# Layer 1 of a conv-attention hybrid: token sums of chunks added during the attention units, and work moved between the two linear parts

## The chip, the cores and the metric

The kernel runs on one core of one Trainium2 chip. The metric is the device time in microseconds of one execution, and the number compared is the median of several runs.

## What is computed

The input is eight images of 384 channels and 32 x 32 positions, that is 1024 tokens of 384 numbers per image. Layer 0 normalises groups of channels and adds an attention of 8 heads with a relative bias. Layer 1, which the change touches, works on the tokens of layer 0's output:

```python
t = t + attn(_ln_t(t))        # 6 heads of 64; q and k normalised per head and token
t = t + ffn(_ln_t(t))         # 384 -> 1536 -> 384, gelu between, both linear parts quantised

def _ln_t(v, eps=1e-5):
    m = jnp.mean(v, axis=-1, keepdims=True)
    s = jnp.var(v, axis=-1, keepdims=True)
    return (v - m) / jnp.sqrt(s + eps)
...
for g in range(NUM_GROUPS):   # 5 groups over 8 images: one image each, the last three give zero
    gamma = jnp.max(jnp.abs(ag))
    xq = xq.at[...].set(jnp.clip(ag * QB / (gamma + EPS), -QB + EPS, QB - EPS))
```

So only images 0 to 4 have a feed-forward part; for images 5 to 7 it adds nothing, and the kernel leaves it out. The normalisation of tokens (`_ln_t`) needs, for each token, the sum over 384 channels of the values and of their squares. The quantisation of the first linear part needs the largest absolute value of the whole image before gelu can start.

## The kernel before

An image lies in SBUF channel by channel: three chunks of 128 channels on the partitions, 1024 tokens along each row. A sum over channels is therefore a sum over partitions and chunks, and the kernel makes it on TensorE, with a matrix of ones as the weights (`token_sums`, L1112 to L1130). For each of the three chunks it multiplies x and the square of x, each in two halves of 512 tokens. The four results use 32 columns of the array each. All three chunks accumulate in one PSUM tile. In f32 every such product shows as two matmul records. ScalarE makes the squares (`square`, L1107). The sums go through DRAM into a layout with tokens on the partitions (two DMAs on SyncE's queue, SP), and GpSimd makes mean and scale from them (`token_stats`, L1133).

There are two such sums per image: the a-sum ("tsa") on the image that comes next, for its attention, where only the scale is needed, and it is applied to v late; and the f-sum ("tsf") on the image after its attention, for the feed-forward part.

The attention of an image runs in 24 units (3 pairs of heads x 2 halves of the queries x 4 groups of keys, L1611). In each unit TensorE makes scores (`scores`, L1286), ScalarE takes exp of them, and VectorE adds up the exps for the softmax's divisor. Two units later (`LAG`) TensorE multiplies them with v (`weigh`, L1331). When a pair of heads is done, `divide` (L1359) sums over keys, inverts, spreads the result by DMA ("rb") and multiplies the output oT by it.

Between the units of two images lies a seam. After images 5 and 6 the seam holds only the next image's projections (`attention_inputs`, L1583): the a-sum, q and k of three pairs, the last units' products, and four quarters of v, which VectorE scales with the a-sum's result as it takes them from PSUM (L1240). The output projection of the old image follows behind unit 3 of the next.

After images 0 to 4 the seam holds much more, written out by hand in the main loop from L1671 on. In TensorE's order: the four quarters of v for the next image (`project_v`, L1225) with the last products between them; the output projection (`project_out`, L1395), whose last pair needs rb; q of pair 0 (`project(0, 0)`); the f-sum, the a-sum; k of pair 0, q of pair 1, sums of q and k over each head (`head_sums`, L1173), k of pair 1; the first linear part ("y1p", L1481), 12 row blocks of 12 matmuls; q and k of pair 2; the second linear part ("y2p", L1538), 12 steps k of 12 matmuls. Both linear parts work on two float32r parts of each value, a high and a low one. For the first, `layer_norm` (L1421) makes them on VectorE and ScalarE after the f-sum has gone through DRAM and GpSimd. For the second, `Supply.gelu` and `Supply.split` (L1522 to L1533) make them on ScalarE and VectorE, chunk by chunk, once `quant_scale` has the largest value.

`normalise_qk` (L1186) turns head sums into scales: SP loads them, GpSimd takes a power, SP stores them and loads the k scales; after `steps[0]` more steps SP spreads the q scales ("rq"), and `steps[1]` steps later VectorE multiplies q by them.

Three things set the order. Each engine runs its instructions in the order in which the program issues them. `_Later` (L64) keeps work that is due after so many calls of `step()`; a call comes after each unit, each projection, each row block and each step k, and what is due is issued there. And buffers are few: PSUM has four tiles of 128 x 1024 for everything (`mm2`, L111), and the f32 work tiles of that size (`wtile`) are 16.

Of the kernel before, what the change touches and what calls it, by code (L numbers as in the profile page):

```python
# [27 lines left out]
P = 128  # L28
# [3 lines left out]
KC = C // P  # L32
# [998 lines left out]
def _layer1(tc, ins, x1, out, shared, start, before=None, check=None):  # L1031
# [4 lines left out]
    with ExitStack() as ctx:  # L1036
# [75 lines left out]
        def token_sums(name, xt, sqs):  # L1112

            pst = mm2("ts" + name)
            for k in range(KC):
                for i, s in enumerate((xt[:, k], sqs[k])):
                    for h in range(NH):
                        nc.tensor.matmul(
                            pst[ts(2 * i + h, 32), 0], ones[:, 0:32], s[:, ts(h, HALF)],
                            start=(k == 0), stop=(k == KC - 1),  # L1120
                        )
# [21 lines left out]
        def project_qk(b, pair, s, xt, dst, sq, step=True):  # L1143
# [3 lines left out]
            for k in range(KC):  # L1147
                for h in range(NH):
                    nc.tensor.matmul(  # L1149
                        pq[:, h], wqkv[:, k, s * C + pair * P : s * C + (pair + 1) * P],  # L1150
                        xt[:, k, ts(h, HALF)], start=(k == 0), stop=(k == KC - 1),
                    )
# [72 lines left out]
        def project_v(b, xt, m2, c=None):  # L1225
# [9 lines left out]
            if c is None:  # L1235
                nc.vector.tensor_copy(v[:, 2 * m2 : 2 * m2 + 2], pv[:, :, 0:C])
# [158 lines left out]
        def project_out(b, oT, xt, then):  # L1395

            pps = []
            for pairs in (range(NP1 - 1), range(NP1 - 1, NP1)):
                for m in range(KC):
# [81 lines left out]
        def feed_forward_1(b, un, between):  # L1481
# [17 lines left out]
            for m in range(FC):  # L1499
# [7 lines left out]
                if m == 4:  # L1507
                    between()
            top = largest(f"1_{b}", parts)
            quant_scale(top)  # L1510
            return y1, top
# [26 lines left out]
        def feed_forward_2(b, supply, between, xt):  # L1538
# [10 lines left out]
            for k in range(FC):  # L1549
                supply.split(k + 1)  # L1550
                supply.gelu(k + 2)
# [3 lines left out]
                between(k)  # L1555
                later.step()
# [26 lines left out]
        def attention_inputs(b, xt, rest=()):  # L1583
# [3 lines left out]
            tk = token_sums(f"a{b}", xt, [square(f"a{b}", xt, k) for k in range(KC)])  # L1587
# [40 lines left out]
        for b in range(B):  # L1628
# [9 lines left out]
            for i, u in enumerate(units):  # L1638
# [7 lines left out]
                if i == 3:  # L1646
# [4 lines left out]
                    ahead = load(b + 1) if more else None  # L1651
            if not more:
# [6 lines left out]
            if not ffn:  # L1659

                def last(i, b=b, oT=oT, held=held):
                    weigh_last(b, oT, held[i])
                    if i == 1:
                        divide(b, oT, NP1 - 1)

                nqk, nkc = attention_inputs(b + 1, ahead, [lambda: last(0), lambda: last(1)])
# [3 lines left out]
            else:  # L1670
                nqk, sq, d, nkc = {}, {}, head_rows(b + 1), kc_tile(b + 1)  # L1671
                sqs = [square(f"a{b + 1}", ahead, k) for k in range(KC)]

                def project(pair, s, step=True):
# [122 lines left out]
```

## Time and profile before

| what | us |
|---|---|
| median of 3 runs (lowest 3085.49, highest 3087.35) | 3085.55 |
| the profiled execution | 3085.19 |
| its span, from first to last instruction | 3083.4 |
| TensorE busy with matmuls | 3039.7 |
| VectorE, ScalarE, GpSimd busy | 1736.9, 1400.0, 472.1 |
| layer 1's first matmul of a token sum starts at | 1434.1 |

A line of the profile's timeline gives the start in us, the us that the entry spans, the engine (PE is TensorE, DVE VectorE, ACT ScalarE, POOL GpSimd, SP SyncE), the source line, the operation, the tiles written and read, their shapes and the number of instructions. A bracket at its end gives the time that the engine stood idle before it and who ended that. A matmul's record is longer than the pace of the matmuls, since the next one starts before its end: 128 x 512 f32 records have a mean of 596 ns and start 0.43 us apart. So a busy TensorE can still hold small losses, and they are read from the starts.

TensorE's longest waits for a named releaser in layer 1, over the whole span (us, times, longest):

```
PE y2p L1544 <- DVE ly L1533: 5.3, 9, 0.7
PE hs L1178 <- ACT qsq L1165: 3.3, 5, 0.7
PE y2p L1544 <- ACT qsq L1165: 3.0, 5, 0.6
PE pp L1404 <- DVE oT L1390: 2.4, 1, 2.4
PE s L1293 <- DVE v L1240: 2.2, 2, 1.2
PE y1p L1490 <- ACT qsq L1165: 2.2, 5, 0.4
PE y1p L1490 <- DVE lun L1444: 2.1, 5, 0.4
PE tsa L1118 <- ACT tsqa L1109: 1.5, 2, 0.8
```

### The profile page before, as it was taken

The numbers are of one execution on the slowest core, as the hardware profiler recorded it, in microseconds if no ns is written. First come the engines' busy times: TensorE is split into PE (matmuls) and PEld (weight loads), VectorE is DVE, ScalarE is ACT, GpSimd is POOL, SyncE is SP. The second block draws the span as 40 slices with busy tenths as digits, with TensorE's granted clock in tenths as the row PEclk, the third lists the DMA queues.
The fourth block names the chain that finished last, engine by engine and source line by source line (L and its number), as shares of the span: only waits on it lengthen the run. The fifth ranks groups of instructions, "written<-read, shape, count | busy, mean of one in ns | idle before, by whom it ended". The sixth has DMA issues, their size and how long they took to land.

```text
span 3083.4 us, 45983 instructions
## 1 busy us (share of the span) xinstructions
PE 3039.7 (99%) x19066; PEld 1582.6 (51%) x19066; DVE 1736.9 (56%) x1735; ACT 1400.0 (45%) x1763; POOL 472.1 (15%) x315
## 2 busy tenths in 40 slices
PE   8999999999999999999999999999999999999998
PEld 3455546454555546444545555645645645634343
DVE  3846547273646547263645845745745745745545
ACT  2634426162434526153644643543643544544534
POOL 0111102011111102032201301201201201211110
PEclk9999999999999999999999999999999999999999
DMA  7402020202112020213301101101101101102011
GB/s 185 115 19 82 20 80 23 82 18 50 51 25 82 19 81 23 57 66 95 81 15 30 56 15 30 57 15 30 57 15 30 57 15 30 57 9 73 14 51 44
DMA packets 102771, 150.51 MB, mean 49 GB/s; under 512 B 62260, under 2 KB 65828, under 8 KB 101784
## 3 DMA queue, kind: packets, MB, share of 16 engines
q1 hardware_dynamic: 99688, 147.41, 16.8%
q8 instruction: 153, 2.51, 0.3%
q14 instruction: 66, 0.54, 0.1%
q10 hardware_dynamic: 2864, 0.05, 0.1%
HBM read 111.05 MB, written 27.32 MB: 45 GB/s over the span
## 4 chain that ended last, share of the span: by engine, by line
PE 87%; DVE 4%; DMA 3%; ACT 2%; issue 1%; SPq 1%; POOL 1%; DVEq 0%; ACTq 0%; POOLq 0%
PE s L521 14%; PE o L552 14%; PE s L1293 11%; PE o L1342 10%; PE pq L467 8%; PE y2p L1544 5%; PE pp L616 4%; PE y1p L1490 4%; PE pp L1404 4%; PE pv L495 4%; PE pq L1149 4%; PE pv L1230 3%; SPq L391 1%; PE sum L1365 1%; POOL hc L1199 1%
## 5 line engine op out<-in xcount | busy, mean ns | idle before, releaser
L536 ACT ACTIVATE e<-e 128x1024 f32<-128x1024 f32 x512 | 535.0, 1057 | 442.7 <-DVE e L532 422.1
L532 DVE TENSOR_TENSOR e<-s,grow 128x1024 f32<-128x1024 f32 x512 | 601.4, 1218 | 190.4 <-PE s L521 189.8
L521 PE MATMUL s<-qk 48*64 48x512 f32 x4096 | 612.4, 592 | 2.7 <-DVE e L532 2.6
L552 PE MATMUL o<-e,v 64*64 64x512 f32 x4096 | 608.3, 590 | 0.0
L1304 ACT ACTIVATE e<-s,kc 128x512 f32<-128x512 f32 x768 | 463.4, 691 | 200.1 <-PE s L1293 183.9
L1293 PE MATMUL s<-qk,qk 64*64 64x512 f32 x3072 | 393.1, 592 | 2.4 <-DVE v L1240 2.2
L1342 PE MATMUL o<-e,v 64*64 64x512 f32 x3072 | 390.8, 591 | 0.0
L521 PEld LDWEIGHTS s<-qk 48*64 48x64 f32 x4096 | 237.0, 132 | 228.5 <-issue 76.3
L552 PEld LDWEIGHTS o<-e,v 64*64 64x64 f32 x4096 | 259.6, 133 | 178.4 <-issue 71.1
L1319 DVE TENSOR_TENSOR t<-t,e 128x1024 f32<-128x1024 f32 x192 | 231.1, 1222 | 75.3 <-ACT e L1304 75.2
L1149 PE MATMUL pq<-bx,wqkv 128*128 128x512 f32 x576 | 254.1, 596 | 0.7 <-ACT tra L1123 0.7
L467 PE MATMUL pq<-xn,w 128*128 128x512 f32 x576 | 250.7, 596 | 0.0
L581 POOL TENSOR_TENSOR inv<-sums,over 128x16 f32<-128x16 f32 x32 | 92.7, 2898 | 1008.7 <-DMA sums<-sd 850.1
L1293 PEld LDWEIGHTS s<-qk,qk 64*64 64x64 f32 x3072 | 142.8, 132 | 200.2 <-issue 124.3
L1342 PEld LDWEIGHTS o<-e,v 64*64 64x64 f32 x3072 | 137.4, 133 | 192.7 <-issue 165.8
L467 PEld LDWEIGHTS pq<-xn,w 128*128 128x128 f32 x576 | 109.2, 191 | 142.3 <-issue 139.5
L1149 PEld LDWEIGHTS pq<-bx,wqkv 128*128 128x128 f32 x576 | 107.8, 190 | 143.5 <-issue 141.4
L1316 DVE TENSOR_TENSOR t<-e,e 128x1024 f32<-128x1024 f32 x96 | 114.1, 1224 | 71.4 <-ACT e L1304 71.2
L1477 DVE TENSOR_REDUCE parts<-y 128x1 f32<-128x1024 f32 x75 | 90.1, 1218 | 99.1 <-ACT y L1474 98.6
L1165 ACT ACTIVATE qsq<-pq 128x1024 f32<-128x1024 f32 x48 | 49.1, 1024 | 195.5 <-DVE qk L1159 97.3
L1199 POOL TENSOR_TENSOR hc<-hc,rsqrt 128x32 f32<-128x32 f32 x24 | 135.4, 5642 | 2.0
L1230 PE MATMUL pv<-wqkv,bx 128*128 128x384 f32 x384 | 131.0, 497 | 0.0
(151 smaller groups left out, 2936.6 us busy)
## 6 DMA issues: line engine op xcount, KB each, us to landing
rb<-rd SPq DMA_DIRECT2D x112, 256.0 KB
xn<-in_x_dram SPq DMA_DIRECT2D x24, 512.0 KB
res<-in_x_dram SPq DMA_DIRECT2D x24, 512.0 KB
x<-res SPq DMA_DIRECT2D x24, 512.0 KB
bx<-x SPq DMA_DIRECT2D x8, 1536.0 KB
rq<-hi SPq DMA_DIRECT2D x48, 256.0 KB
out_dram<-bx SPq DMA_DIRECT2D x24, 512.0 KB
wide<-table SPq DMA_DIRECT2D x80, 114.2 KB
```

The source lines that it names most:

```text
L467: nc.tensor.matmul(pq[:, h], wqk[:, k, s, 2 * pair : 2 * pair + 2, :].rearrange("p h d -> p (h d)"), xn[:, k, ts(h, HALF)], start=(k == 0) ...
L521: nc.tensor.matmul(s[j][ts(c, QP), i], qk[pair][rows, 1, ts(4 * m2 + 2 * i + c, QP)], qk[pair][rows, 0, ts(h, HALF)], start=True, stop=True,)
L532: nc.vector.tensor_add(e.rearrange("p (i q) -> p i q", i=2), s[j], bass.AP(near.tensor, near.offset, [near.ap[0], [-QROWS * IW, 2], [1, HA ...
L536: nc.scalar.activation(e, e, AF.Exp)
L552: nc.tensor.matmul(po[ts(j, S0), r], v[keys, 2 * m2 + i, 2 * pair + j, :], es[j][keys, ts(i, HALF)], start=(m2 == 0 and i == 0), stop=(m2 ...
L1149: nc.tensor.matmul(pq[:, h], wqkv[:, k, s * C + pair * P : s * C + (pair + 1) * P], xt[:, k, ts(h, HALF)], start=(k == 0), stop=(k == KC - 1),
L1199: nc.gpsimd.tensor_tensor(c, c, rsqrt.to_broadcast(list(c.shape)), ALU.pow)
L1230: nc.tensor.matmul(pv[:, i, 0:C], xt[:, k].rearrange("c (p m) -> c m p", m=MT)[:, 2 * m2 + i], wqkv[:, k, 2 * C : 3 * C], start=(k == 0), ...
L1293: nc.tensor.matmul(s[j][ts(c, QP), i], qk[pair, 1][rows, ts(4 * m2 + 2 * i + c, QP)], qk[pair, 0][rows, ts(h, HALF)], start=True, stop=True,)
L1304: nc.scalar.activation(e[:, ts(i, HALF)], s[j][:, i], AF.Exp, scale=kc[:, pair, j, m : m + 1])
L1319: nc.vector.tensor_add(total[j], total[j], e)
L1342: nc.tensor.matmul(po[ts(j, D1), r], v[keys, 2 * m2 + i, at : at + D1], es[j][keys, ts(i, HALF)], start=(m2 == 0 and i == 0), stop=(m2 == ...
```

## The change

- **Sums of added chunks.** A new function `fold` adds the next image's three chunks into one tile on VectorE, and its three squares (ScalarE) into another. It runs in five stages that are due after units 13, 14, 15, 19 and 20 of the image before, for images 1 to 7. The a-sum then has one chunk instead of three. For the f-sum, chunks 0 and 1 and their squares are added on VectorE after the output projection; it has two chunks. Image 0's a-sum stays as it was.
- **The f-sum stands earlier.** It is issued in the middle of `project(0, 0)`, whose matmuls are put in the order of the two halves for that.
- **The last quarter of v moves** from before the output projection to just ahead of the second linear part, and ScalarE takes it from PSUM instead of VectorE. A `later.step` between the pairs of the output projection takes the place of the moved one there.
- **Normalising q and k of pairs 0 and 1** starts after row blocks 2 and 4 instead of both after block 4, with other step counts.
- **Ahead of the second linear part** q of pair 2 is projected before `quant_scale` and the first gelus; two chunks are split and three gelus issued there instead of one and two, and the loop works one chunk further ahead, after `between(k)` instead of before the products.
- **At the attention-only seams** the multiply by rb is due two steps later, (2, 4) instead of (2, 2).

```diff
             nc.scalar.activation(sq, xt[:, k], AF.Square)
             return sq
-        def token_sums(name, xt, sqs):
+        def chunks(xt):
+            return [xt[:, k] for k in range(KC)]
+        def fold(name, xt):
+            xs, sqs, one = [], [], []
+            def first():
+                sqs.append(square(name, xt, 0))
+                xs.append(wtile("tx" + name))
+                nc.vector.tensor_add(xs[0], xt[:, 0], xt[:, 1])
+            def next_square(k):
+                one.append(square(name, xt, k))
+            def add_square():
+                nc.vector.tensor_add(sqs[0], sqs[0], one.pop())
+            return xs, sqs, [
+                first,
+                lambda: (next_square(1), nc.vector.tensor_add(xs[0], xs[0], xt[:, 2])),
+                add_square,
+                lambda: next_square(2),
+                add_square,
+            ]
+        def token_sums(name, xs, sqs):
             pst = mm2("ts" + name)
-            for k in range(KC):
-                for i, s in enumerate((xt[:, k], sqs[k])):
+            for k in range(len(xs)):
+                for i, s in enumerate((xs[k], sqs[k])):
                     for h in range(NH):
                         nc.tensor.matmul(
                             pst[ts(2 * i + h, 32), 0], ones[:, 0:32], s[:, ts(h, HALF)],
-                            start=(k == 0), stop=(k == KC - 1),
+                            start=(k == 0), stop=(k == len(xs) - 1),
                         )
             rows = wtile("tr" + name, (P, HALF))
             nc.scalar.copy(rows, pst[:, 0])
...
             nc.gpsimd.tensor_scalar(var, var, 1e-5, 0.0, ALU.add, ALU.add)
             nc.gpsimd.tensor_tensor(var, var, rsqrt.to_broadcast([P, MT]), ALU.pow)
-        def project_qk(b, pair, s, xt, dst, sq, step=True):
+        def project_qk(b, pair, s, xt, dst, sq, step=True, middle=None):
             pq = mm2(f"pq{b}_{pair}_{s}")
-            for k in range(KC):
-                for h in range(NH):
-                    nc.tensor.matmul(
-                        pq[:, h], wqkv[:, k, s * C + pair * P : s * C + (pair + 1) * P],
-                        xt[:, k, ts(h, HALF)], start=(k == 0), stop=(k == KC - 1),
-                    )
+            order = [(k, h) for k in range(KC) for h in range(NH)]
+            for k, h in order if middle is None else sorted(order, key=lambda kh: kh[1]):
+                if middle is not None and (k, h) == (0, 1):
+                    middle()
+                nc.tensor.matmul(
+                    pq[:, h], wqkv[:, k, s * C + pair * P : s * C + (pair + 1) * P],
+                    xt[:, k, ts(h, HALF)], start=(k == 0), stop=(k == KC - 1),
+                )
             def take():
                 t = qkp.tile([P, N], F32, tag="qk", name=f"qk{b}_{pair}_{s}")
...
             later.after(steps[0], apply)
-        def project_v(b, xt, m2, c=None):
+        def project_v(b, xt, m2, c=None, copy=nc.vector.tensor_copy):
             pv = mm2(f"pv{b}_{m2}")
             for i in range(2):
...
                         wqkv[:, k, 2 * C : 3 * C], start=(k == 0), stop=(k == KC - 1),
                     )
             if c is None:
-                nc.vector.tensor_copy(v[:, 2 * m2 : 2 * m2 + 2], pv[:, :, 0:C])
+                copy(v[:, 2 * m2 : 2 * m2 + 2], pv[:, :, 0:C])
             else:
                 for i in range(2):
                     m = 2 * m2 + i
...
             later.after(steps[0], invert)
-        def project_out(b, oT, xt, then):
+        def project_out(b, oT, xt, then, between=None):
             pps = []
             for pairs in (range(NP1 - 1), range(NP1 - 1, NP1)):
+                if between is not None and NP1 - 1 in pairs:
+                    between()
                 for m in range(KC):
                     if len(pps) <= m:
                         pps.append(mm2(f"pp{b}_{m}"))
...
                 evict(y, py[m], b1, parts, m, nc.scalar)
                 y1.append(y)
                 later.step()
-                if m == 4:
-                    between()
-            top = largest(f"1_{b}", parts)
-            quant_scale(top)
-            return y1, top
+                between(m)
+            return y1, largest(f"1_{b}", parts)
         class Supply:
...
                         )
             for k in range(FC):
-                supply.split(k + 1)
-                supply.gelu(k + 2)
                 if k < FC - 2:
                     for m in range(KC):
                         products(k, m)
                 between(k)
+                supply.split(k + 2)
+                supply.gelu(k + 3)
                 later.step()
             for m in range(KC):
                 for k in (FC - 2, FC - 1):
...
         def head_rows(b):
             return dram.tile([NP1, 8, HALF], F32, tag="hs", name=f"hd{b}")
-        def attention_inputs(b, xt, rest=()):
+        def attention_inputs(b, xt, rest=(), sums=None):
             d, qk, sq = head_rows(b), {}, {}
             kc = kc_tile(b)
-            tk = token_sums(f"a{b}", xt, [square(f"a{b}", xt, k) for k in range(KC)])
+            if sums is None:
+                sums = chunks(xt), [square(f"a{b}", xt, k) for k in range(KC)]
+            tk = token_sums(f"a{b}", *sums)
             def head(pair, *steps):
                 head_sums(b, pair, sq, d)
...
                         behind = None
                     oT = wide.tile([P, KC, N], F32, tag="o", name=f"oT{b}")
                     ahead = load(b + 1) if more else None
+                    if more:
+                        *ahead_sums, stages = fold(f"a{b + 1}", ahead)
+                        for at, stage in zip((13, 14, 15, 19, 20), stages):
+                            later.after(at - i, stage)
             if not more:
                 for done in held:
                     weigh_last(b, oT, done)
...
                 def last(i, b=b, oT=oT, held=held):
                     weigh_last(b, oT, held[i])
                     if i == 1:
-                        divide(b, oT, NP1 - 1)
-                nqk, nkc = attention_inputs(b + 1, ahead, [lambda: last(0), lambda: last(1)])
+                        divide(b, oT, NP1 - 1, (2, 4))
+                nqk, nkc = attention_inputs(
+                    b + 1, ahead, [lambda: last(0), lambda: last(1)], ahead_sums
+                )
                 behind = lambda b=b, oT=oT, xt=xt: project_out(
                     b, oT, xt, lambda m: store(b, xt, m)
                 )
             else:
                 nqk, sq, d, nkc = {}, {}, head_rows(b + 1), kc_tile(b + 1)
-                sqs = [square(f"a{b + 1}", ahead, k) for k in range(KC)]
-                def project(pair, s, step=True):
-                    return project_qk(b + 1, pair, s, ahead, nqk, sq, step)
+                def project(pair, s, step=True, middle=None):
+                    return project_qk(b + 1, pair, s, ahead, nqk, sq, step, middle)
                 def normalise(pair, *steps):
                     normalise_qk(b + 1, pair, nqk, d, nkc, steps)
...
                     project_v(b + 1, ahead, i)
                     weigh_last(b, oT, held[i])
                 divide(b, oT, NP1 - 1, (1, 1))
-                for m2 in range(2, MT // 2):
-                    project_v(b + 1, ahead, m2)
-                fsq = []
-                project_out(b, oT, xt, lambda m: fsq.append(square(f"f{b}", xt, m)))
-                project(0, 0)
-                fc = token_sums(f"f{b}", xt, fsq)
-                un, normal = layer_norm(b, xt, fc)
-                tk = token_sums(f"a{b + 1}", ahead, sqs)
+                project_v(b + 1, ahead, 2)
+                fsq, fc = [], []
+                project_out(b, oT, xt, lambda m: fsq.append(square(f"f{b}", xt, m)), later.step)
+                two = wtile(f"two{b}")
+                nc.vector.tensor_add(two, xt[:, 0], xt[:, 1])
+                nc.vector.tensor_add(fsq[0], fsq[0], fsq[1])
+                project(
+                    0, 0,
+                    middle=lambda: fc.append(
+                        token_sums(f"f{b}", (xt[:, KC - 1], two), (fsq[KC - 1], fsq[0]))
+                    ),
+                )
+                un, normal = layer_norm(b, xt, fc[0])
+                tk = token_sums(f"a{b + 1}", *ahead_sums)
                 project(0, 1)
                 project(1, 0)
                 head_sums(b + 1, 0, sq, d)
...
                 normal()
                 take()
-                def between_1():
-                    head_sums(b + 1, 1, sq, d)
-                    normalise(0, 5, 6)
-                    normalise(1, 6, 6)
-                supply = Supply(b, *feed_forward_1(b, un, between_1))
+                def between_1(m):
+                    if m == 2:
+                        normalise(0, 5, 2)
+                    elif m == 4:
+                        head_sums(b + 1, 1, sq, d)
+                        normalise(1, 5, 3)
+                y1, top = feed_forward_1(b, un, between_1)
+                project(2, 0)
+                quant_scale(top)
+                supply = Supply(b, y1, top)
                 supply.gelu(0)
                 supply.gelu(1)
-                take = project(2, 0, step=False)
                 supply.split(0)
+                take = project(2, 1, step=False)
+                supply.split(1)
+                supply.gelu(2)
                 take()
-                project(2, 1)
+                project_v(b + 1, ahead, MT // 2 - 1, copy=nc.scalar.copy)
                 def between_2(k):
                     if k == 0:
```

## The prediction

> **What bounds it.** I read the page, then the granted clock (0.999 throughout, so no case rests on it), then TensorE's groups and waits, then the timelines of all engines around the seams between images of layer 1.
>
> ```profile
> PE 3039.7 (99%) x19066; PEld 1582.6 (51%) x19066; DVE 1736.9 (56%) x1735; ACT 1400.0 (45%) x1763; POOL 472.1 (15%) x315
> ```
>
> TensorE sets the end: matmuls taken off it, and waits in front of it, count in full; work on other engines costs only where TensorE then waits. The token sums by shape:
>
> ```profile
> L1118 PE MATMUL tsa<-bx,ones 128*32 128x512 f32 x96 | 22.6, 596 | 0.0
> L1118 PE MATMUL tsf<-bx,ones 128*32 128x512 f32 x60 | 13.8, 596 | 0.0
> ```
>
> With as many for the squares: 24 records per a-sum (8 sums), 24 per f-sum (5). Image 1's seam on TensorE (start us, us, ..., idle before <- who ended it):
>
> ```profile
> 1844.98 5.31 PE L1149 MATMUL pq<-bx,wqkv 128*128 128x512 f32 x12
> 1850.23 0.62 PE L1118 MATMUL tsf<-bx,ones 128*32 128x512 f32 x2
> ...
> 1852.83 0.60 PE L1118 MATMUL tsa<-bx,ones 128*32 128x512 f32 x2
> ...
> 1855.52 10.57 PE L1149 MATMUL pq<-bx,wqkv 128*128 128x512 f32 x24
> ...
> 1879.08 0.73 PE L1490 MATMUL y1p<-lun,w 128*128 128x512 f32 x2 [0.42 <-DVE lun L1444]
> ...
> 1882.10 0.73 PE L1490 MATMUL y1p<-un,w 128*128 128x512 f32 x2 [0.42 <-ACT qsq L1165]
> ...
> 1908.43 10.46 PE L1149 MATMUL pq<-bx,wqkv 128*128 128x512 f32 x24
> 1919.01 0.73 PE L1544 MATMUL y2p<-hy,w 128*128 128x512 f32 x2
> 1920.34 0.72 PE L1544 MATMUL y2p<-ly,w 128*128 128x512 f32 x2 [0.60 <-DVE ly L1533]
> ...
> 1922.59 0.73 PE L1544 MATMUL y2p<-hy,w 128*128 128x512 f32 x2 [0.59 <-ACT qsq L1165]
> ...
> 1924.45 1.07 PE L1178 MATMUL hs<-qsq,heads 128*32 128x512 f32 x8 [0.66 <-ACT qsq L1165]
> ...
> 1926.90 0.72 PE L1544 MATMUL y2p<-ly,w 128*128 128x512 f32 x2 [0.71 <-DVE ly L1533]
> ```
>
> A chunk of a sum is 8 records, four side by side: (1852.83 - 1850.23) / 3 = 0.87 us. A projection is 5.2, a y pair 0.23 per matmul. From 1908.43 to 1926.90 is 18.5 us; unbroken it is 10.46 + 12 x 0.233 + 1.0 + 0.47 = 14.7. The same stretch of the five images gives 17.8, 18.5, 17.9, 18.0, 17.6: a loss of 3.2 in the mean. The other seam (image 5 to 6; 6 to 7 is like it):
>
> ```profile
> 2733.47 1.05 PE L1118 MATMUL tsa<-bx,ones 128*32 128x512 f32 x4
> 2735.30 0.62 PE L1118 MATMUL tsa<-tsqa,ones 128*32 128x512 f32 x2 [0.77 <-ACT tsqa L1109]
> ...
> 2738.17 15.72 PE L1149 MATMUL pq<-bx,wqkv 128*128 128x512 f32 x36
> ```
>
> The sum takes 4.7 us there instead of 2.6, for its three squares are only made after the last exps. These waits are few, but behind them stands all that TensorE does next, so each ends up in the span.
>
> **1. Sums at the two attention-only seams.** One chunk instead of three, its squares made 10 us earlier: 4.7 to 0.9, gain 3.8. The multiply by rb moves behind the last v (2,4): before, DVE stood at it from 2789.4 to 2795.0 with v's scaling (L1240) queued behind, and TensorE waited 1.23 and 1.01. Then exp of unit 0 becomes the limit (scores 2 need its PSUM tile, about 2797.5 against 2798.0 now): I take 0.7, between 0.3 and 1.2. Sum 2 x 4.5 = 9.0.
>
> **2. Sums at the five feed-forward seams.** tsa loses two chunks, 1.73; tsf one, 0.87. But the f-sum now stands in mid-projection, 2.6 us after project_out. DVE's last residual add ended 1.4 us after it (1846.47), `two` and the square add follow at 1.22 each (row of L1436): 3.9 us, while TensorE wants the added squares at 3.5: 0.4 lost. Splitting the projection also adds two changes of array shape. The Trainium skill (TensorEngine Tiling (Array Packing), Key Properties) says that a change of tiling mode drains TensorE. Rows: the last of 12 projections starts near 1849.70 and tsf at 1850.23, 0.53 where 0.43 is the pace, so 0.1 a change; a full drain by the matmul's 0.60 would be 0.17. That makes 0.2 (row) or 0.35 (rule); I take 0.25. Net 2.60 - 0.4 - 0.25 = 1.95 (between 1.5 and 2.4).
>
> **3. The layer norm and the first linear part.** Its chain (sums, POOL, DMAs) took 14.1 us from 1853.13 to DVE's start at 1867.26, and starts 3.2 us earlier relative to project_out's end. But DVE does the copy of pq(1,0) first, as now, and that comes with TensorE. Its chain of nine multiplies and subtractions then runs 11.8 us (1867.26 to 1879.02), and pq(1,1)'s copy (1.99) and square (1.02) follow it before the fourth y1p gets its PSUM tile. So both waits there (loss 1.9 us from 1871.86 to 1882.10 against 36 x 0.232) stay but shrink, as TensorE has 24.7 us of work from project_out to y1p and DVE starts 0.3 earlier against it: gain 0.35 (0 to 1.0).
>
> **4. Ahead of the second linear part.** Let T be the first part's end (1908.43). Last quarter of v now follows the two projections: pq(2,0) to T+5.2, pq(2,1) to T+10.4, v to T+14.4 (12 records, 4.03). DVE: pq(2,0) copied by T+6.5; then later.step runs pair 1's multiply by rq (5 + 3 steps end there), to T+7.65; quant_scale (ready at T+6.7) to T+8.25. ACT: table load 1.28, gelu 0 to T+10.75, gelu 1 to 11.8, gelu 2 to 12.9. DVE: split 0 (0.69 + 1.22) to 12.8, split 1 to 14.7, transposing copy of pq(2,1) (1.94) to 16.6; ACT square to 17.65, v's copy (768 columns; 512 took 0.58, 1024 took 1.02, so 0.8) to 18.5. So y2p k=0 has its operands at T+14.4 and runs m=0 and 1 (0.93 each). The four PSUM tiles go round: now y2p m=2 waits for the tile of pq(2,0), two accumulators back (the wait on qsq at 1922.59). With v between, m=2 gets pq(2,1)'s tile, wanted at 16.3 and free at 17.7: 1.4 lost. Head sums need the tile of v's copy, 18.5, wanted at 18.65. Splits two chunks ahead end the ly wait. Loss 3.2 becomes 1.4: gain 1.8, between 0 (hr's DMA, as now, holds a work tile of split 2 as well) and 3.0.
> Pair 1's rq is behind hd, hc, hi, two kc and rq of pair 0 on SP; POOL ended that pair's power at 1908.87, now not later, since pair 0's (5.4 us) is moved ahead of it. rq so lands about T; DVE has 6 us of cover, and each us beyond it costs one, with quant_scale and both splits queued behind it.
>
> **5. The pv moved out of project_out's front.** 4.03 us, neither gained nor lost, but it was cover. rb's multiply ended 13.8 to 14.1 us after the softmax sum's start; TensorE now wants it after 1.0 + 4.0 + 10.3 = 15.3. The step between the pairs keeps its place on DVE. Cost nothing, cover 1.2; without it, us for us.
>
> **6. In the units.** Three squares (three take 2.96, 0.95 each), four adds (1.22) per image, 7 images. ACT in image 1's units 13 and 14:
>
> ```profile
> 1771.06 2.42 ACT L1304 ACTIVATE e<-s,kc 128x512 f32<-128x512 f32 x4 [0.96 <-PE s L1293]
> 1773.35 0.60 ACT L1351 COPY oT<-o 128x512 f32<-128x512 f32 x1
> 1774.49 2.42 ACT L1304 ACTIVATE e<-s,kc 128x512 f32<-128x512 f32 x4 [0.54 <-PE s L1293]
> ```
>
> In unit 13 a square in a gap of 0.54 delays the next exp by 0.4; TensorE's next scores need half of that exp 0.25 later: 0.2 lost. Units 14 and 19 have a gap of 1.0 and lose nothing. DVE falls 2.4 us behind by unit 15 and recovers in 16, which has no adds. The rule of table sets (ScalarE: Activation LUTs, Table sets) would charge two loads a square if Square and Exp were of different sets, some 50 us of ACT in all; the trace shows squares straight behind exps (1809.12 and 2734.17) with no load. I take -0.2 x 7 = -1.4 (0 to -4).
>
> **Sum.** 5 x (1.95 + 0.35 + 1.8) + 9.0 - 1.4 = 28.1. The profiled execution took 3085.19 (span 3083.4 and 1.8 around it): 3057.1. The median of the runs is 0.36 above it: 3057.5.
>
> **Rivals.** *Waits move* (0.18): the y2p gain is 0, its third PSUM tile or a work tile coming late: 28.1 - 9.0 = 19, so 3066.5. For it: DVE and ACT run pq(2,1)'s readers after both splits. Against it: hy and ly are ready long before. *Waits vanish* (0.16): no stall at tsf, y1p gains 1.0, y2p 3.0: 5 x (2.35 + 1.0 + 3.0) + 10.0 = 41.8, so 3043.8. For it: 4 us more TensorE work covers the chain. Against it: the PSUM tile above. *Slower* (0.04): b_work has 16 tiles. I count 11 in use in the units (6 e, 2 totals, 2 folded, 1 row); xs, sqs and one square, held from unit 13, make 14. If tiles ran out, exp would wait for the products two units back, 1.7 us after its scores: with 0.25 of slack 1.4 per unit, 10 units, 7 images, 98 us, so 3155; it decides from 0.4 us per unit on (28 / 70). Against it: exps now wait on scores alone (183.9 us), never on a tile. *Change does not tell* (0.02): the seams pay back all.
>
> **Numbers.** The forecast has 0.60. The range takes in both near rivals, 3043 to 3069; the forecast's own is 3050 to 3064. A measurement here tells 0.2% (6 us) from no change: faster 0.94, within 0.02, slower 0.04.
>
> **What would show it.** tsa of 8 records and about 0.9 us at the two attention-only seams, without a wait on tsqa; tsf with a short wait on DVE; y2p's ly waits gone and one wait of about 1.4 on qsq at m=2; scores in unit 15 late by 0.2. Wrong if scores wait on exps in many units, if y2p waits on rq or v's copy, or pp on rb.

## The result and the profile after

| what | before | after |
|---|---|---|
| median of 5 runs, us | 3085.49 (3082.79 to 3087.35) | 3058.54 (3056.22 to 3058.97) |
| the profiled execution, us | 3085.19 | 3058.54 |
| its span, us | 3083.4 | 3056.7 |

The ratio after to before is 0.9911, with a 95% interval of 0.9899 to 0.9922. The forecast was 3057.5. The time is right. That it came so close is in part luck, since the errors of two terms nearly cancel; and for the second linear part the runs show a cause that the sum did not have.

The first part of the page after, busy time by engine: TensorE runs 152 matmul records fewer and is 15.8 us less busy; the other 11 us of the span's 26.7 are waits and the gaps between records.

```profile
PE 3023.9 (99%) x18914; PEld 1595.5 (52%) x18914; DVE 1771.8 (58%) x1768; ACT 1401.7 (46%) x1768; POOL 463.0 (15%) x315
```

TensorE's timeline at image 1's seam (the same seam that the prediction showed of before):

```profile
1840.87 2.74 PE L1178 MATMUL pq<-bx,wqkv 128*128 128x512 f32 x6
1843.54 0.62 PE L1145 MATMUL tsf<-bx,ones 128*32 128x512 f32 x2
...
1844.42 0.60 PE L1145 MATMUL tsf<-two,ones 128*32 128x512 f32 x2
1844.68 0.62 PE L1145 MATMUL tsf<-tsqf,ones 128*32 128x512 f32 x2
...
1845.66 2.84 PE L1178 MATMUL pq<-bx,wqkv 128*128 128x512 f32 x6
1848.43 0.62 PE L1145 MATMUL tsa<-txa,ones 128*32 128x512 f32 x2
...
1849.43 10.57 PE L1178 MATMUL pq<-bx,wqkv 128*128 128x512 f32 x24
...
1872.99 0.73 PE L1521 MATMUL y1p<-lun,w 128*128 128x512 f32 x2 [0.41 <-DVE lun L1475]
...
1875.99 0.73 PE L1521 MATMUL y1p<-un,w 128*128 128x512 f32 x2 [0.43 <-ACT qsq L1194]
...
1912.61 4.03 PE L1259 MATMUL pv<-wqkv,bx 128*128 128x384 f32 x12
1916.19 0.92 PE L1572 MATMUL y2p<-hy,w 128*128 128x512 f32 x2
...
1919.30 0.72 PE L1572 MATMUL y2p<-hy,w 128*128 128x512 f32 x2 [0.79 <-ACT qsq L1194]
```

The a-sum is one chunk (1848.43 to 1849.43). The added squares of the f-sum come 0.24 late: at TensorE's pace their records would start 0.02 behind those of `two`, like the pairs before them. The two y1p waits are the old ones, 0.42 each. Of the four y2p and head-sum waits one is left, 0.79 at m = 2, where the prediction had put it.

To place the gain I cut TensorE's timeline of layer 1 into stretches between the starts of matmul records. Means over images 0 to 4, in us:

| stretch | before | after |
|---|---|---|
| units, first scores to the first pv | 83.12 | 83.34 |
| first pv to output projection | 21.11 | 17.24 |
| output projection | 15.45 | 15.45 |
| q of pair 0 to first y1p (the sums lie here) | 26.88 | 24.90 |
| first linear part, to T | 36.57 | 36.55 |
| T to first y2p | 10.08 | 13.87 |
| first y2p to the next image's scores | 38.33 | 36.09 |

The quarter of v moves 3.9 us from the second row to the sixth, so these two and the last are one sum: 69.52 before, 67.20 after. At the attention-only seams the a-sum fell from 4.7 to 1.00 and the stretch from scores 0 to the output projection from 12.45 and 12.23 to 11.57 twice.

So the account, image by image: sums 5 x 1.98 = 9.9; first linear part 5 x 0.02 = 0.1; v and second part 5 x 2.32 = 11.6; attention-only seams 2 x 3.7 + 0.88 + 0.66 = 8.9; units of seven images -1.4. That is 29.1 for layer 1. Layer 0, whose code is the same, ended 2.8 us later in this run (layer 1's first scores at 1495.85 instead of 1493.08). The sum is 26.3, the spans differ by 26.7.

### The profile page after: what moved, and what is told of

The parts are those of the page before. It is cut to its first block, busy times and chain, and to the rows that moved or that the text cites. A ratio compares the mean times of both kernels' runs of the same rounds, so it can differ in the third digit from the quotient of the medians.

```text
span 3056.7 us, 45678 instructions
## 1 busy us (share of the span) xinstructions
PE 3023.9 (99%) x18914; PEld 1595.5 (52%) x18914; DVE 1771.8 (58%) x1768; ACT 1401.7 (46%) x1768; POOL 463.0 (15%) x315
## 4 chain that ended last, share of the span: by engine, by line
PE 92%; DVE 3%; DMA 2%; ACT 1%; SPq 1%; issue 1%; ACTq 0%; DVEq 0%
PE o L552 15%; PE s L521 15%; PE s L1322 11%; PE o L1371 10%; PE pq L467 8%; PE pq L1178 7%; PE y2p L1572 5%; PE pp L616 4%; PE y1p L1521 4%; PE pp L1435 4%; PE pv L1259 4%; PE pv L495 4%; PE sum L1394 1%; DVE qk L1188 1%; PE hs L1207 1%
## 5 line engine op out<-in xcount | busy, mean ns | idle before, releaser
L521 PE MATMUL s<-qk 48*64 48x512 f32 x4096 | 605.8, 591 | 2.3 <-DVE e L532 2.2
L552 PEld LDWEIGHTS o<-e,v 64*64 64x64 f32 x4096 | 257.9, 133 | 182.6 <-issue 80.9
L1371 PEld LDWEIGHTS o<-e,v 64*64 64x64 f32 x3072 | 148.1, 133 | 180.7 <-issue 142.7
L477 DVE TENSOR_SCALAR qk<-pq,bqk 128x1024 f32<-128x1024 f32 x24 | 30.8, 1284 | 177.6 <-PE pq L467 177.6
```

What stands on the lines that cost most here:

```text
L521: nc.tensor.matmul(s[j][ts(c, QP), i], qk[pair][rows, 1, ts(4 * m2 + 2 * i + c, QP)], qk[pair][rows, 0, ts(h, HALF)], start=True, stop=True,)
L552: nc.tensor.matmul(po[ts(j, S0), r], v[keys, 2 * m2 + i, 2 * pair + j, :], es[j][keys, ts(i, HALF)], start=(m2 == 0 and i == 0), stop=(m2 ...
L1371: nc.tensor.matmul(po[ts(j, D1), r], v[keys, 2 * m2 + i, at : at + D1], es[j][keys, ts(i, HALF)], start=(m2 == 0 and i == 0), stop=(m2 == ...
```

## The experiments

Each starts from the kernel after. The ratios are to the kernel before, run beside each; after has 0.9911. Several of their intervals touch that of after, so where a few us matter, the stretches decide.

| kernel | median us | ratio, 95% |
|---|---|---|
| old order ahead of the second part (e1) | 3058.89 | 0.9912 (0.9895 to 0.9928) |
| three chunks again (e2) | 3075.94 | 0.9968 (0.9956 to 0.9979) |
| quant_scale first (e3) | 3056.74 | 0.9906 (0.9889 to 0.9922) |
| pair 1's copies on ScalarE (e4) | 3051.04 | 0.9890 (0.9874 to 0.9907) |
| f-sum behind the projection (e5) | 3060.93 | 0.9913 (0.9896 to 0.9929) |
| rb early (e6), one run | 3056.49 | |
| e1 with a late small power on GpSimd (e7) | 3072.35 | 0.9949 (0.9933 to 0.9966) |
| adds one unit later (e8), one run | 3058.06 | |
| gelus first (e10) | 3053.80 | 0.9887 (0.9871 to 0.9904) |
| e10 and e4 together (e11) | 3046.00 | 0.9862 (0.9846 to 0.9879) |

**Old order.** The last quarter of v back ahead of the output projection, the old order, copies and splits ahead of the second part; the new starts of the normalising (row blocks 2 and 4) stay.

```diff
...
-                project_v(b + 1, ahead, 2)
+                for m2 in range(2, MT // 2):
+                    project_v(b + 1, ahead, m2)
...
-                project(2, 0)
                 quant_scale(top)
...
+                take = project(2, 0, step=False)
                 supply.split(0)
-                take = project(2, 1, step=False)
-                supply.split(1)
-                supply.gelu(2)
                 take()
-                project_v(b + 1, ahead, MT // 2 - 1, copy=nc.scalar.copy)
+                project(2, 1)
```

> The changed kernel with the old order around the second linear part: last quarter of v ahead of the output projection, quant_scale at once, one chunk split and two gelus ahead, splits one step ahead. The earlier power of pair 0 on GpSimd is kept. Theory A (the order pays): all of the 2.3 us per image that this stretch gained comes back, 5 x 2.3 = 11.6 us, about 3070. Theory B (what pays is that the largest value comes 3.4 us earlier from GpSimd, since its power is done earlier): the projections alone then cover the chain, the first split stands ready, only the second one is late by about 0.8 us, so +1 to +3 us, about 3060.

The gain did not go. The three stretches sum to 66.99, against 67.20 after and 69.52 before. With the new starts of the normalising in place, the new order adds nothing (-0.2). Of what stayed, those starts bear on this stretch (the sums lie ahead of it), and the traces show three things that come with them.

The first is that GpSimd is free. Its timeline before, at the same seam:

```profile
1903.45 5.41 POOL L1199 TENSOR_TENSOR hc<-hc,rsqrt 128x32 f32<-128x32 f32 x1
1914.76 0.38 POOL L1463 PARTITION_ALL_REDUCE qt<-qm  x1 [5.90 <-issue]
```

And after:

```profile
1887.54 5.42 POOL L1228 TENSOR_TENSOR hc<-hc,rsqrt 128x32 f32<-128x32 f32 x1
1905.21 0.38 POOL L1494 PARTITION_ALL_REDUCE qt<-qm  x1 [12.26 <-DVE qm L1492]
```

The reduce (of the largest value, in `quant_scale`) wants `qm`. Before, `qm` was there at 1911.20 by the chain of waits, but the reduce started at 1914.76, 5.90 after pair 1's power ended, and the bracket names nobody. After, and in e1, the power ended 12 us before the reduce, which started as soon as `qm` was there. In the mean of the five images e1's reduce starts 2.84 us sooner after T than before's.

The second is the load of gelu's table. ScalarE before:

```profile
1915.78 1.28 ACT L1524 ACT_TABLE_LOAD   x1 [6.05 <-DVE qt L1470]
1917.08 2.19 ACT L1524 ACTIVATE y<-y,qt 128x1024 f32<-128x1024 f32 x2
```

And in e1:

```profile
1908.08 1.28 ACT L1552 ACT_TABLE_LOAD   x1
1910.64 2.19 ACT L1552 ACTIVATE y<-y,qt 128x1024 f32<-128x1024 f32 x2 [1.28 <-DVE qt L1501]
```

Before, the load itself waits for `qt` at all five seams; in e1 it runs while `qt` is still being made, which is worth 1.32 us more. Why the wait stands in a different place is not shown. The first gelu so starts 3.96 us after T instead of 8.12, in the mean.

The third is VectorE's split of chunk 1. Before, its low part waits for the head sums, 1.03 to 1.05 us at each of the five seams; in e1 that wait is gone:

```profile
1925.62 1.23 DVE L1533 SCALAR_TENSOR_TENSOR ly<-y,hy 128x1024 fp32r<-128x1024 f32 x1 [1.03 <-PE hs L1178]
```

A work tile is the likely reason: by the code `rq` of pairs 0 and 1 holds one each until its multiply, and pair 0's multiply comes 22.8 us after T before and 1.7 us ahead of T in e1. This was not tried by itself.

**Late power.** e1, and a small power on GpSimd after row block 10, whose result nobody reads (an added instruction).

```diff
                 between(m)
+                if m == 10:
+                    late = small.tile([P, 8], F32, tag="late", name=f"late{b}")
+                    nc.gpsimd.tensor_tensor(
+                        late, parts[:, 3:11], rsqrt.to_broadcast([P, 8]), ALU.pow
+                    )
```

> The old order around the second linear part (e1) with one small instruction more: after row block 10 GpSimd takes a power of 128 x 8 of the largest values into a tile that nobody reads. By the rows of such a power it takes 1.7 us and ends about 1.4 us behind the end of the first linear part (T). Theory (what the change gained ahead of the second linear part is GpSimd's rest before the reduce: behind a power it starts 5.9 us after it, after a rest at once): the reduce starts at about T+7 instead of T+2.9, and the 2.3 us per image come back, with 1 more: +12 to +17 us against e1's 3058.9, so 3071 to 3076. Rival (the reduce's 3.6 us of delay came from the place of the normalisation's DMAs, not from GpSimd's own work): no change, 3059.

GpSimd's timeline in this kernel:

```profile
1907.75 1.63 POOL L1541 TENSOR_TENSOR late<-parts,rsqrt 128x8 f32<-128x8 f32 x1 [10.05 <-DVE parts L1508]
1915.19 0.38 POOL L1494 PARTITION_ALL_REDUCE qt<-qm  x1 [5.80 <-issue]
```

The reduce again starts 5.80 after the last GpSimd instruction, and the three stretches sum to 69.52. Against e1 the median rose by 13.5 us (the kernel before, run beside each, differs by 1.1), 2.5 per image of it in these stretches. One instruction of 1.6 us on a nearly idle engine, read by nobody, costs as much as the change had gained at the second linear part.

That the sum is the one of before is chance, though. The reduce is 5.25 us later than in e1 here, in the mean, and was only 2.84 later before; the table is loaded ahead of `qt` here, and the split of chunk 1 does not wait. What e7 does show is the price of a late gelu: in its five images the first gelu starts 8.96 to 9.41 us after T, and the stretches sum to 60.3 us more than that each time. Carried on to smaller values (an estimate from these five images), e1's order would bear a first gelu up to 6.65 us after T, where the sum is e1's 67.0. The reduce alone, as late as before's, would then cost about 0.15 of the 2.5 us, the reduce and the table load together about 1.5, and the other 1.1 fit the wait of the split. So by these rows the old order's loss has three causes, and only the reduce was tried by itself, in a larger dose.

Nor does e1 show that the new order is worthless. After, `qt` is not what the gelus wait for. VectorE and then ScalarE after:

```profile
1909.93 0.15 DVE L1499 TENSOR_SCALAR qt<-qt 128x1 f32<-128x1 f32 x1
```

```profile
1908.92 1.02 ACT L1194 ACTIVATE qsq<-pq 128x1024 f32<-128x1024 f32 x1 [5.29 <-DVE qk L1186]
1909.96 1.28 ACT L1552 ACT_TABLE_LOAD   x1
1911.26 3.23 ACT L1552 ACTIVATE y<-y,qt 128x1024 f32<-128x1024 f32 x3
```

The gelus stand behind the square of pq(2,0) and the table load, which ends after `qt` is done (1910.46). VectorE itself starts on `qt` only 7.6 us after T (1902.31), behind a copy and a multiply. Before, the reduce had ended by 6.7 us after T at the latest, so it would have been in time here, and e3 below, which has `qt` 4.3 us earlier, gains nothing. By these rows the new order and the earlier start each do the work alone. The new order with the old start was not run.

**Three chunks again.** The a-sum and the f-sum of three chunks each, squares at the seams, no adds in the units.

```diff
-                        *ahead_sums, stages = fold(f"a{b + 1}", ahead)
...
                     middle=lambda: fc.append(
-                        token_sums(f"f{b}", (xt[:, KC - 1], two), (fsq[KC - 1], fsq[0]))
+                        token_sums(f"f{b}", chunks(xt), fsq)
                     ),
...
-                tk = token_sums(f"a{b + 1}", *ahead_sums)
+                tk = token_sums(f"a{b + 1}", chunks(ahead), sqs)
```

> The changed kernel without the added chunks: both sums have three chunks again, squares of the next image are made at the seam, nothing is added in the units; the f-sum keeps its new place. Theory (sums count in full on TensorE): per feed-forward seam tsa +1.73 and tsf +0.87, less the 0.24 us that tsf waits for VectorE now, 5 x 2.35 = 11.8; attention-only seams 2 x 3.8 = 7.6; units -0.2 x 7 = -1.4; in all +18, about 3076. Rival (the added chunks only shift waits to the y1p chain and to the units): +9 or less, about 3067.

The median rose by 17.4 us. The stretch with the sums is 27.21 (after 24.90), the attention-only a-sums are 4.69 and 4.70 again, with their two waits of 0.8 on `tsqa`. The added chunks are worth about what the prediction gave them.

**quant_scale first.** quant_scale ahead of q of pair 2, the gelus left where they are.

```diff
-                project(2, 0)
                 quant_scale(top)
+                project(2, 0)
```

> The changed kernel with quant_scale issued ahead of the projection of q of pair 2, so that it stands ahead of that copy and of the multiply by rq on VectorE. Theory (the wait of y2p at m=2 is VectorE's queue: copy, multiply, quant_scale, two splits, copy of pq(2,1)): everything up to the splits comes 4 us earlier, pq(2,1) is copied by T+15.6 and the wait goes: -0.9 x 5 = -4.5 us, about 3054. Rival (the PSUM tile is held by ScalarE, whose gelus and squares take as long): no change.

Every stretch is that of after within 0.06. ScalarE's timeline in this kernel shows why: gelu (L1552) and its table stand behind the square of pq(2,0), which waits for the projection.

```profile
1908.32 1.02 ACT L1194 ACTIVATE qsq<-pq 128x1024 f32<-128x1024 f32 x1 [5.29 <-DVE qk L1186]
1909.36 1.28 ACT L1552 ACT_TABLE_LOAD   x1
1910.65 3.23 ACT L1552 ACTIVATE y<-y,qt 128x1024 f32<-128x1024 f32 x3
```

**Gelus first.** quant_scale and two gelus ahead of the projection's copy and square; split(0) between its matmuls and its copy.

```diff
-                project(2, 0)
                 quant_scale(top)
                 supply = Supply(b, y1, top)
                 supply.gelu(0)
                 supply.gelu(1)
+                take = project(2, 0, step=False)
                 supply.split(0)
+                take()
+                later.step()
                 take = project(2, 1, step=False)
```

> The changed kernel with quant_scale and gelus 0 and 1 ahead of the projection of q of pair 2, so that on ScalarE too nothing of that projection stands ahead of them, and q of pair 2 taken after split 0. Theory (the wait left at y2p m=2 is the in-order queue: in e3 ScalarE held the table load and gelus behind the square of pq(2,0)): split 0 ends about T+8, pq(2,1) is copied by T+14.4 and squared by T+15.4, before TensorE wants its tile at T+16.3: -0.9 x 5 = -4.5, about 3054. Rival: another wait takes its place (head sums on v's copy, or the splits on the multiply by rq): no change.

ScalarE's timeline in this kernel:

```profile
1900.82 1.28 ACT L1552 ACT_TABLE_LOAD   x1
1903.38 2.19 ACT L1552 ACTIVATE y<-y,qt 128x1024 f32<-128x1024 f32 x2 [1.28 <-DVE qt L1501]
1907.76 1.02 ACT L1194 ACTIVATE qsq<-pq 128x1024 f32<-128x1024 f32 x1 [2.19 <-DVE qk L1186]
```

The table is loaded while the engine waits for `qt`, and the gelus run in time that it stood idle before. The y2p wait on `qsq` is gone from TensorE's waits, and the last stretch is 35.04 instead of 36.09, 5.2 us over five images; the median is 4.7 below after's.

**Copies on ScalarE.** q and k of pair 1 taken from PSUM by ScalarE instead of VectorE (`project_qk` gets the copy as an argument).

```diff
-                project(1, 0)
+                project(1, 0, copy=nc.scalar.copy)
...
-                    take = project(1, 1, step=False)
+                    take = project(1, 1, step=False, copy=nc.scalar.copy)
```

> The changed kernel with q and k of pair 1 taken from PSUM by ScalarE instead of VectorE at the feed-forward seams. Theory (both waits inside y1p are VectorE's queue: the copy of pq(1,0) ahead of the layer norm's chain and the copy of pq(1,1) behind it): the chain starts about 1.2 us earlier and the PSUM tile comes free 2 us earlier, y1p loses 0.3 instead of 1.9 us: -1.6 x 5 = -8 us, about 3050. Rival (the chain starts when its two DMAs land, and ScalarE's casts are delayed by the copies): no change or +2 us.

The first linear part takes 34.95 instead of 36.55 and both y1p waits are gone: 8.0 us over five images, 7.5 in the median. Two copies moved together, so what each is worth is not shown.

**Both.** e10 and e4 in one kernel.

> e10 together with e4 (ScalarE takes q and k of pair 1 from PSUM). If both causes are right and independent, the gains add: -4.5 - 7.5 = -12 us against the changed kernel, about 3046.5; if ScalarE becomes the bound with both, about 3051 as e4 alone.

The gains add: 12.5 us below after, and no y1p or y2p wait is left. It beats both kernels.

**f-sum behind the projection.** The f-sum after the whole of q of pair 0 instead of in its middle.

```diff
-                project(
-                    0, 0,
-                    middle=lambda: fc.append(
-                        token_sums(f"f{b}", (xt[:, KC - 1], two), (fsq[KC - 1], fsq[0]))
-                    ),
-                )
+                project(0, 0)
+                fc.append(token_sums(f"f{b}", (xt[:, KC - 1], two), (fsq[KC - 1], fsq[0])))
```

> The changed kernel with the f-sum behind the whole projection of q of pair 0 instead of in its middle. Theory (the place in the middle is cover for the layer norm's chain, which takes 14.1 us from the sum to VectorE): TensorE saves the 0.24 us of waiting and about 0.2 us of array changes, but the chain ends 2.5 us later against it and the y1p blocks wait: +1 to +2.5 us per image, 5 to 12 in all, so 3064 to 3070. Rival (the chain has slack, since VectorE first takes pq(1,0)): -0.4 x 5 = -2, 3056.5.

Both theories missed the size. In images 0 to 3 the sums' stretch is 0.60 shorter (0.27 for the wait on the added squares, the other 0.33 for the way into the other array shape and out of it) and the first linear part 0.83 longer, a loss of 0.23 each. In image 4 the first y1p waits too, the sums' stretch is 25.11, and the loss is 1.17. That is 2.1 us in all, and 2.4 in the median, which the intervals alone could not tell from nothing. Half of it comes from one seam, so the middle placing is worth between 1 and 2 us.

**rb early.** The multiply by rb due as before at the attention-only seams.

```diff
-                divide(b, oT, NP1 - 1, (2, 4))
+                divide(b, oT, NP1 - 1)
```

> The changed kernel with the multiply by rb due two steps earlier again at the attention-only seams, (2, 2). Theory (v's scaling queued behind it held TensorE's scores): the wait of scores on v comes back, about 1.2 us each, of which 0.5 us per seam counts (as e2's remainder says), +1 us in all, to be read from the stretch of images 5 to 7 (413.9 us), not from the whole time. Rival: the earlier sums made room and it costs nothing.

TensorE's waits in this kernel (total us, times, longest) have the old row again:

```profile
PE s L1322 <- DVE v L1269: 2.2, 2, 1.3
```

The stretches are 12.49 and 12.19, against 11.57: the step is worth 1.5 for both seams. Its one run is 2 us below after's median, which cannot tell this.

**Adds one unit later.** The stages of `fold` after units 14, 15, 16, 19, 20.

```diff
-                        for at, stage in zip((13, 14, 15, 19, 20), stages):
+                        for at, stage in zip((14, 15, 16, 19, 20), stages):
```

> The changed kernel with the first three stages of the added chunks one unit later (14, 15, 16, 19, 20), so that no square falls into unit 13, where ScalarE also copies an accumulator. Theory (a square in a gap of 0.54 us is what the units lose): the units of images 2 to 4 take 82.67 us again instead of 82.83, -0.16 x 7 = -1 us in all. Rival (VectorE's adds cost it): no change.

The units of images 2 and 3 take 82.66 instead of 82.83 (before, image 2: 82.67): what stood in unit 13 costs the 0.2 that was predicted. An add on VectorE moved with the square, so which of them costs it is not shown. Image 4 takes 82.94, so a better place in all images is not shown either.

## Why the prediction was right or wrong

**Part 1 held.** 9.0 predicted, 8.9 measured: a-sum 4.7 to 1.00, rb 0.88 and 0.66 where 0.7 was taken.

**Part 2 held.** 1.95 per image predicted, 1.98 measured. Two of its sizes erred in opposite directions: the wait on the added squares costs 0.27, not 0.4, and the two changes of array shape cost 0.33 (e5), not 0.25. The prediction's figure by the drain, 0.35, was the better one. Its row gave 0.2 because it holds only the gap at the change: on the way back the next matmul, too, starts 0.53 behind the one before it, where 0.43 is the pace.

**Part 3 failed in size: 0.35 predicted, 0.02 measured.** The step was "DVE starts 0.3 earlier against it". VectorE's first subtraction of the layer norm stands behind its copy of pq(1,0), which comes with TensorE, and y1p follows TensorE just the same. VectorE's timeline after:

```profile
1860.03 1.23 DVE L1186 COPY qk<-pq 128x1024 f32<-128x1024 f32 x1 [3.23 <-PE pq L1178]
1861.17 1.22 DVE L1467 TENSOR_TENSOR un<-bx,lc 128x1024 f32<-128x1024 f32 x1
```

And before:

```profile
1866.12 1.23 DVE L1157 COPY qk<-pq 128x1024 f32<-128x1024 f32 x1 [3.23 <-PE pq L1149]
1867.26 1.22 DVE L1436 TENSOR_TENSOR un<-bx,lc 128x1024 f32<-128x1024 f32 x1
```

From 1861.17 to the first y1p (1865.77) is 4.60 us; before it was 1867.26 to 1871.86, also 4.60. The prediction had written that the copy comes first and then still credited the earlier sums. Experiment e4 shows what it takes: with the copy off VectorE the chain starts on the DMA itself, 2.5 us earlier than in the kernel after, counted from the start of q of pair 0.

```profile
1855.95 1.23 DVE L1467 TENSOR_TENSOR un<-bx,lc 128x1024 f32<-128x1024 f32 x1 [1.83 <-DMA lc<-lr]
```

**Part 4 held for the new order, 1.8 predicted and 2.32 measured, but its account of the old loss was incomplete.** What it said of the new order came true: the ly waits are gone, and one wait is left at m = 2, 0.79 where 1.4 was computed. The mis-sized term is the table load. The sum put it behind `qt`, with gelu 0 ending at T+10.75; in the trace the load starts 0.5 us before `qt` is done and gelu 0 ends at T+10.1, and the square that y2p waits for ends 0.7 us earlier than computed.

The incomplete step is the account of the 3.2 us lost before. It was put on PSUM tiles and splits, because these end the waits in TensorE's timeline, and the late start of everything behind `qt` was not asked about. So the sum did not see that the earlier normalising, by itself, takes the loss away: e1 has none of the new order and keeps 2.5. The view was there. In the chain of waits of before:

```profile
1911.03 0.18 DVE qm L1461
1911.20 3.56 issue
1914.76 0.39 POOL qt L1463
```

3.56 us in which the chain waits for nothing that the profile shows, on an engine with 15% busy, is a row to explain (the other four images have 2.7 to 3.1). In the change, pair 0's normalising starts behind row block 2 and no longer with pair 1's behind block 4; pair 1's power, which ended 0.43 us after T, now ends 9.3 us ahead of it (1892.96, T at 1902.31). SP's rows before suggest why: pair 1's head sums were loaded at 1901.12, straight behind the two loads of k scales of pair 0 that SP issued from 1899.30 on. This was not tried by itself. The prediction spoke of that power only as "not later".

What the 5.9 us are: between the power and the reduce the trace has two MODIFY_POOL_CONFIG records 0.2 us behind the power's end, and then nothing. The Trainium skill (GPSIMD Engine Reference, 2.1 Instruction dispatch) says that the first call to a freshly loaded GpSimd kernel pays about 6 us for loading its code, with no instruction to see. From the second of these records to the reduce it is 5.65 us here and 5.55 in e7, near that figure; the trace itself does not show the load. What the traces show is the timing: the ten late reduces of before and e7 start 5.66 to 5.90 us after the instruction ahead of them, and in all runs those with 6.8 us or more of rest start 0.14 to 0.21 us after `qm`.

**Part 5 held.** No new wait of pp on rb.

**Part 6 held.** -1.4 predicted and measured; e8 finds 0.17 per image in what stood in unit 13.

**What was not in the sum** is layer 0's 2.8 us. Its code is unchanged. The windows of the profile for 78 to 92 us (busy time of each engine, then the granted clock, the DMA share and GB/s), before:

```profile
78.00:92.00 14.00, 12.22 (x86) 4.17 (x90) 11.00 (x11) 9.66 (x11) 0.00 (x0) 0.88 0.84 215
```

And after:

```profile
78.00:92.00 14.00, 10.26 (x61) 3.32 (x61) 9.24 (x10) 7.53 (x9) 0.00 (x0) 0.76 0.85 221
```

The granted clock is 0.76 there instead of 0.88. The trace has it at half speed for 6.8 us instead of 3.4, behind a wait of some 2 us for the first exps, and that costs some 1.7 us more (0.12 x 14). The experiments, whose layer 0 is the same code, show both: with 0.88 layer 1's first scores start between 1492.5 and 1493.2 (e2, e5, e6, e10), with 0.76 between 1493.5 and 1496.0 (e1, e3, e4, e7, e8). But e11 has 0.88 and starts at 1496.35. So layer 0 varies by up to 3.8 us between executions, the clock is a part of it, and the rest is not explained.

So 28.1 predicted against 26.7 measured in the spans is 1.7 too much in part 3 (5 x 0.33), 2.6 too little in part 4, and 2.8 for layer 0. Some 0.5 is left, 0.3 of it in image 7. That the errors in parts 3 and 4 nearly cancel is luck. A forecast of e1 by the same reasons (3057.5 and the 9.0 of part 4 given back) would have been 7.6 us too high.

## What to carry to other kernels

A stretch of "issue" in the chain of waits on an idle engine is a cost with an owner: ask what that engine did before it and how long ago, not only how busy it is. When a change bundles an order with a start time, undo each of them alone: undoing one shows only what it adds to the other, and here either may do the work. An experiment that brings the old time back has the old cause only if its dose is the old one. An earlier operand gains nothing while the engine that takes it first copies something that comes with the bottleneck; move that copy (7.5 us here, with a second one).

## What the runs showed of the hardware

- A partition all-reduce on GpSimd that followed other GpSimd work closely started 5.7 to 5.9 us after it (ten reduces in before and e7). With 6.8 us of rest or more it started 0.14 to 0.21 us after its operand.
- The load of gelu's table (1.28 us) can run while its activation still waits for an operand (e10: loaded at 1900.82, gelu at 1903.38). In the kernel before, the load itself stood behind that wait at all five seams.
- The way into the array shape of 32 columns and back cost 0.33 us (e5 against after, images 0 to 3).
- A TensorE busy for 99% of the span still ran at half clock for 3.4 or 6.8 us near 80 us, with a mean granted clock of 0.88 or 0.76 over 14 us, by the execution.
